# Turning the rounded values by block transposes and plain DMAs, and other places for early and last steps, in a fused attention and feed-forward kernel

## The chip, the cores and the metric

The kernel runs on one core of a Trainium2 chip. The time is that of the whole execution on the device in microseconds (us). The engines are TensorE (PE; PEld is its weight load), VectorE (DVE), ScalarE (ACT), GpSimd (POOL) and SyncE (SP), which here only issues DMAs. Each engine works through its own list of instructions in order; semaphores tie the lists together.

## The reference

The input x holds 16 sequences of 256 tokens with 256 channels. All is float32 except where said.

```
x = x + attention(layernorm(x))     16 query heads, 4 key/value heads of 128, softmax over
                                    the first 4 keys and the last 32, then the product with wo
x = x + ffn(layernorm(x))           one 256 x 256 linear layer in rounded integers:
  x_scale = max(max|h| / 127, 1e-12)      per token
  x_q = clip(round(h / x_scale), -128, 127)
  y = (x_q . w_q) * x_scale * w_scale + bias
```

The rounded integers fit bfloat16 exactly, so their product runs in bfloat16 on TensorE with sums in float32.

## The kernel before

**Tiling.** A sequence is two tiles of 128 tokens. A unit is one sequence, one group of four query heads and one tile: 8 units per sequence, 128 in all. The main loop goes once per unit; one pass is called a slot here. A slot's place in its sequence is its number modulo 8.

**Order.** Nothing is left to a scheduler: the function in_written_order (line 21) keeps every engine's instructions in the order in which Python writes them. What is done in a slot besides its own unit is put into lists by the function at (line 826): small (run at the end of the slot, and from unit 125 on, by line 938, already ahead of the normalisation), begin (after the scores), close (in the last unit) and others for keys, values, queries and the output projection.

**One slot.** TensorE makes the scores pss (line 560), a part of the output projection py (L678), the product po of the weights of two units earlier with the values (L623), in some slots the keys or values of the next sequence (pk L495, pv L507) and a pair of query heads (pq L527). Queries, keys, values and output projection go by a scheme with seven products instead of eight, so that VectorE or GpSimd must combine sums (lines 306 to 310, function combine). The query products of a slot lie in two PSUM banks; VectorE empties them in the next slot, L306 and L307 the first, L308 to L310 the second, and the queries of that slot are written to the same banks. VectorE further masks the scores (L571), takes their maximum (L573), normalises after ScalarE's exponentials (L605 to L617) and turns the weights in blocks of 32 x 32 (L582). A DMA out (zd, L584) and a DMA back (ad, L588) finish the turn; po reads ad two slots later. In the last units the turn is done by TensorE instead (ptd, L565), with a wait in the next slot.

**The steps of the rounded layer** (function ffn_steps, line 695, sequences 0 to 14): stats; norm (h = normalised x, L193); scale (xs, L714 and L715); quantise (L719 to L725: multiply and add a large constant on VectorE, clip and subtract it on GpSimd, result h16 in bfloat16); turn (L728, one DMA transpose by SP); linear (pa on TensorE L739, y on VectorE L744, the sum with x on GpSimd L745, the store on SP L746). They run in the next sequence's slots 4, 5, 6, 8, 9 and 10 after the sequence is done, so linear stands in slot 2 modulo 8, and norm, scale in 5 and 6. Sequence 14 has its own places near the end, and a seventh step that adds the bias (L733). The last sequence is done tile by tile (function last_steps, line 750): its d is rounded on VectorE (L778 to L784), turned by TensorE (ht_last, L791), multiplied (pa_last), scaled and stored.

**Turning the normalised x** (function turned_by_blocks, line 385, sequences 2 to 15): VectorE turns 32 x 32 blocks (L389), four DMAs write them to DRAM (L394) and four read them back into place (L403).

**Buffers.** x tiles rotate through 5 buffers (line 74); h, h16, hT and y have one each.

## Time and profile before

| | us |
|---|---|
| median of 3 runs (lowest, highest) | 769.09 (767.9, 769.29) |
| the profiled execution | 767.44 |
| its span, first to last instruction | 765.7 |
| TensorE busy in the span | 754.4 |
| VectorE | 621.8 |
| GpSimd | 511.7 |
| ScalarE | 399.2 |

The mean granted TensorE clock was 0.997. "Busy" counts the time in which an instruction runs; matmuls are pipelined, so two that follow each other overlap in the list. In the timelines a row has its start, its length, the engine, the line, the operation, out<-in by the program's names, shapes and a count; a bracket at the end tells how long the engine was idle before it, and what ended that.

### The profile page before, as it was taken

What the parts mean: (1) busy time and instruction counts of PE and PEld (TensorE: products, weight loads), DVE (VectorE), ACT (ScalarE), POOL (GpSimd) and SP (SyncE); (2) the same over time, 40 slices, a digit from 0 to 9 for tenths busy, and PEclk for the clock granted to TensorE, in tenths of its full rate; (3) what the DMA queues carried; (4) which work ended last, traced back from release to release, by engine and by line L of the source; (5) the groups of instructions that cost most, each with busy time, mean ns of one, the idle gap of its engine ahead of it and who ended that gap; (6) DMA issues with size and microseconds to landing.
All of it is one profiled execution on the core that took longest, in us unless ns stands there. A gap on an engine that the chain in (4) does not pass through costs nothing.

```text
span 765.7 us, 18824 instructions
## 1 busy us (share of the span) xinstructions
PE 754.4 (99%) x6483; PEld 742.4 (97%) x6483; DVE 621.8 (81%) x1775; ACT 399.2 (52%) x1561; POOL 511.7 (67%) x812
## 2 busy tenths in 40 slices
PE   9999999999999999999999999999999999999995
PEld 7999999999999999999999999999999999999994
DVE  2588888888888888888888888888888888778765
ACT  3555555555455454555555455554545555455551
POOL 4666977676675867757676675866758676675622
PEclk9999999999999999999999999999999999999998
DMA  7634354344544425445344543436344354443310
GB/s 241 215 102 129 106 147 140 107 124 118 154 124 133 131 90 163 128 137 144 100 125 128 147 141 123 129 96 163 120 145 135 99 136 128 130 137 105 100 40 31
DMA packets 150679, 97.45 MB, mean 127 GB/s; under 512 B 44984, under 2 KB 148792, under 8 KB 150584
## 3 DMA queue, kind: packets, MB, share of 16 engines
q1 hardware_dynamic: 150584, 96.24, 42.8%
q8 instruction: 52, 0.85, 0.5%
q14 instruction: 43, 0.35, 0.2%
HBM read 54.39 MB, written 39.85 MB: 123 GB/s over the span
## 4 chain that ended last, share of the span: by engine, by line
PE 96%; DVE 2%; DMA 1%; ACT 0%; POOL 0%; issue 0%; DVEq 0%; POOLq 0%; ACTq 0%
PE pq L527 24%; PE py L678 23%; PE po L623 15%; PE pss L560 14%; PE pk L495 6%; PE pv L507 6%; PE py L662 3%; PE pq L538 2%; PE pa L739 1%; DMA ad<-zd 1%; PE warm L891 1%; PE pv L470 0%; PE pk L461 0%; PE ptd L565 0%; ACT scores L598 0%
## 5 line engine op out<-in xcount | busy, mean ns | idle before, releaser
L598 ACT ACTIVATE scores<-scores,nmax 128x68 f32<-128x68 f32 x512 | 173.5, 340 | 247.2 <-DVE nmax L573 244.8
L623 PE MATMUL po<-ad,vw 96*128 96x128 f32 x1024 | 135.4, 275 | 0.4 <-DMA ad<-zd 0.4
L560 PE MATMUL pss<-kt,qt 128*128 128x68 f32 x1024 | 130.2, 268 | 0.0
L623 PEld LDWEIGHTS po<-ad,vw 96*128 96x128 f32 x1024 | 125.6, 192 | 1.5 <-DMA ad<-zd 0.5
L560 PEld LDWEIGHTS pss<-kt,qt 128*128 128x128 f32 x1024 | 126.1, 192 | 0.7 <-issue 0.5
L527 PE MATMUL pq<-xs,wq_sums 128*128 128x128 f32 x714 | 118.6, 275 | 0.0
L571 DVE SCALAR_TENSOR_TENSOR scores<-pss,masks 128x272 f32<-128x272 f32 x128 | 56.2, 439 | 63.7 <-PE pss L560 60.8
L527 PEld LDWEIGHTS pq<-xs,wq_sums 128*128 128x128 f32 x714 | 98.8, 192 | 0.0
L598 ACT ACTIVATION_READ_ACCUMULATOR scores<-scores,nmax 128x1 f32 x512 | 95.6, 187 | 0.0
L635 ACT COPY oT<-po 128x512 f32<-128x512 f32 x129 | 75.4, 585 | 23.0 <-PE po L623 23.0
L678 PE MATMUL py<-wo_sums,os 128*128 128x128 f32 x672 | 87.0, 279 | 0.0
L257 POOL TENSOR_TENSOR os<-oT 128x256 f32<-128x256 f32 x56 | 41.0, 732 | 58.0 <-ACT oT L635 58.0
L678 PEld LDWEIGHTS py<-wo_sums,os 128*128 128x128 f32 x672 | 79.5, 192 | 0.0
L306 POOL TENSOR_TENSOR ktmp<-b_k 128x256 f32<-128x256 f32 x30 | 22.4, 746 | 84.3 <-ACT b_k L327 84.3
L527 PE MATMUL pq<-xnT,wq_sb 128*128 128x128 f32 x476 | 72.7, 275 | 0.1
L582 DVE STREAM_TRANSPOSE z<-scores 128x384 f32<-128x384 f32 x120 | 69.4, 578 | 4.1
L617 DVE TENSOR_TENSOR scores<-scores,sm 128x272 f32<-128x272 f32 x120 | 60.3, 503 | 4.1
L527 PEld LDWEIGHTS pq<-xnT,wq_sb 128*128 128x128 f32 x476 | 62.7, 192 | 0.2 <-PE pv L507 0.2
L678 PE MATMUL py<-wo_sb,oT 128*128 128x128 f32 x448 | 62.0, 281 | 0.0
L573 DVE TENSOR_REDUCE nmax<-scores 128x4 f32<-128x272 f32 x128 | 55.8, 436 | 4.4
L678 PEld LDWEIGHTS py<-wo_sb,oT 128*128 128x128 f32 x448 | 54.5, 192 | 0.0
L308 DVE TENSOR_TENSOR qt<-pq,qt 128x256 f32<-128x256 f32 x119 | 50.5, 424 | 4.0
(187 smaller groups left out, 1700.4 us busy)
## 6 DMA issues: line engine op xcount, KB each, us to landing
zd<-z SPq DMA_DIRECT2D x120, 192.0 KB
ad<-zd SPq DMA_DIRECT2D x120, 192.0 KB
vd<-vt SPq DMA_DIRECT2D x30, 256.0 KB
vw<-vd SPq DMA_DIRECT2D x30, 256.0 KB
vw<-vd SPq DMA_DIRECT2D x30, 224.0 KB
x<-in_x_dram SPq DMA_DIRECT2D x15, 256.0 KB
out_dram<-y SPq DMA_DIRECT2D x15, 256.0 KB
zxd<-zx SPq DMA_DIRECT2D x56, 64.0 KB
```

The costliest lines, as they stand in the source:

```text
L308: eng.tensor_add(c21_c22, like(p[1][:, 0:2], c21_c22), v.unsqueeze(1).to_broadcast(c21_c22.shape))
L495: pe.matmul(to, left, right, start=True, stop=True)
L527: pe.matmul(to, left, right, start=True, stop=True)
L560: pe.matmul(pss[:, k, :], qt[n, g][:, t, k].rearrange("p h i -> p (h i)"), kt[n, g][:, t * NBLK + k, :], start=True, stop=True,)
L571: dve.scalar_tensor_tensor(s[:, :, 0:NK], pss, SCALE, masks[:, t], ALU.mult, ALU.add)
L573: dve.tensor_reduce(nmax, s[:, :, 0:NK], AX.X, ALU.max, negate=True)
L582: dve.transpose(z, s.rearrange("p k (c i) -> p c k i", c=NCH))
L598: act.activation(s[:, k, 0:NK], s[:, k, 0:NK], AF.Exp, bias=nmax[:, k : k + 1], scale=1.0, accum_out=sm[:, k : k + 1],)
L617: dve.tensor_mul(s, s, sm.unsqueeze(2).to_broadcast([P, NBLK, NK]))
L623: pe.matmul(po[:, k], vw[n, g // 2][:, t * NBLK + k, g % 2 * D : (g % 2 + 1) * D], ad[:, :, k], start=True, stop=True,)
L635: act.copy(o[:, t, hs].rearrange("p h (k i) -> p k h i", i=QB), po[:, :, hs])
L678: pe.matmul(region(py, i), left[:, e], right[:, e], start=(g == 0 and e == 0 and i in (1, 4)), stop=(g == G - 1 and e == 1 and i in (7, 3)),)
```

## The change

Four things change.

1. For sequences 0 to 13 the rounded values are no longer turned by one DMA transpose of a bfloat16 tile. They stay float32 (h, clipped and shifted in place), and go the way of the normalised x: a block transpose on VectorE, four DMAs out, four back (turned_by_blocks, made general), and a copy on ScalarE that narrows to bfloat16 (narrow). The steps are nine now, at slots 4, 5, 6, 8, 10, 11, 12, 13, 14 after the sequence's end; for sequence 13 at 4, 5, 6, 8, 9, 10, 11, 12, 13. The linear step so moves from slot 2 to slot 6 modulo 8, and to unit 125 for sequence 13. x tiles get a sixth buffer.
2. Sequence 14's values are turned by four bfloat16 transposes on TensorE.
3. In the last unit the matmuls of sequence 14's linear step are issued where they were, but their scaling, sum and store (rest) come after the rounding of the last sequence's first tile. x2's copy is issued earlier, and for the first tile its bias is added on GpSimd.
4. Early steps: the first sequence's transposes are copied out by halves on two engines, one half of sequence 2's norm moves from slot 5 to 6, and the rounding of the layer's weights from slot 9 to 8.

```diff
-    xp = ctx.enter_context(tc.tile_pool(name="xp", bufs=5))
+    xp = ctx.enter_context(tc.tile_pool(name="xp", bufs=6))
...
-    def turned_by_blocks(n):
+    def turned_by_blocks(src, pool_of, tag):
-        dve.transpose(z, xns[n].rearrange("p t (c q i) -> p q (t c) i", c=NC, q=NQ))
+        dve.transpose(z, src.rearrange("p t (c q i) -> p q (t c) i", c=NC, q=NQ))
...
-            (act.copy, dve.tensor_copy)[j](xnT[n][:, :, j * P : (j + 1) * P], pt)
+                (act.copy, dve.tensor_copy)[c](xnT[n][:, c, j * P : (j + 1) * P], pt[:, c])
...
-        h16 = p1.tile([P, NT, DM], BF, tag="h16", name=f"h16_{tag}")
+        h16 = p1.tile([P, NT, DM], BF, tag="h16", name=f"h16_{tag}") if n == B - 2 else h
...
+        way = []
+
         def turn():
-            sp.dma_start_transpose(
-                hT.rearrange("p j c t -> p (j c) t"), h16.rearrange("p j d -> p (j d)")
-            )
+            if n < B - 2:
+                way.extend(turned_by_blocks(h, p1, f"hb_{tag}"))
+                return
+            pt = ps_m.tile([P, NC, T], BF, tag="m", name=f"ht_{tag}")
+            for c in range(NC):
+                for j in tiles:
+                    pe.transpose(pt[:, c, j * P : (j + 1) * P], h16[:, j, c * P : (c + 1) * P], ident16)
+            way.append(pt)
+
+        def out():
+            way[0]()
+
+        def back():
+            way.append(way[1]())
+
+        def narrow():
+            act.copy(hT, way[-1])
...
-            for j in tiles:
-                dve.scalar_tensor_tensor(y[:, j, :], pa[:, j, :], xs[:, j : j + 1], wsc_bc, ALU.mult, ALU.mult)
-            pool.tensor_add(y, y, xt)
-            sp.dma_start(out_v[n], y)
+            def rest():
+                for j in tiles:
+                    dve.scalar_tensor_tensor(y[:, j, :], pa[:, j, :], xs[:, j : j + 1], wsc_bc, ALU.mult, ALU.mult)
+                pool.tensor_add(y, y, xt)
+                sp.dma_start(out_v[n], y)
+
+            return rest
-        return [stats, norm, scale, quantise, turn, linear, lambda: add_bias(dve)]
+        if n < B - 2:
+            return [stats, norm, scale, quantise, turn, out, back, narrow, linear]
+        return [stats, norm, scale, quantise, turn, narrow, linear, lambda: add_bias(dve)]
...
-            if j:
-                act.copy(x2, py)
+            act.copy(x2, py)
...
+            if j == 0:
+                pool.tensor_add(x2, x2, bias_bc)
...
-        places = (0, 1, 1, 2) if n == 1 else (4, 5, 6, 7) if n == 2 else (first - 2, first + 2, first + 4, first + 5)
+        places = (0, 1, 1, 2) if n == 1 else (4, 6, 6, 7) if n == 2 else (first - 2, first + 2, first + 4, first + 5)
...
-    for slot, f in zip((6, 9, 10, 10, 11, 12), ffn_weight_steps()):
+    for slot, f in zip((6, 8, 10, 10, 11, 12), ffn_weight_steps()):
...
-        slots = (4, 5, 6, 8, 9, 10) if n < B - 2 else (4, 5, 6, 6, 7, 7, 7)
+        slots = (4, 5, 6, 8, 10, 11, 12, 13, 14) if n < B - 2 else (4, 5, 6, 6, 7, 7, 7, 7)
+        if n == B - 3:
+            slots = (4, 5, 6, 8, 9, 10, 11, 12, 13)
         for k, slot in enumerate(slots):
-            def step(n=n, k=k):
+            def step(n=n, k=k, slot=done + slot):
                 if k == 0:
                     steps[n] = ffn_steps(n)
-                steps[n][k]()
-            at(done + slot, step, begin if k == 4 and n == B - 2 else close if k == 5 and n == B - 2 else small)
+                rest = steps[n][k]()
+                if rest and n == B - 2:
+                    at(slot, rest, close)
+                elif rest:
+                    rest()
+            if n < B - 2:
+                at(done + slot, step, begin if k in (5, 6) else small)
+            else:
+                at(done + slot, step, begin if k == 4 else close if k == 6 else small)
...
             tail = last_steps(0)
             for f in tail[:2]:
                 f()
+            for f in close.pop(i):
+                f()
```

More of the change, by code (lines that the diff above doesn't have):

```diff
@@ L383, in turned @@
         channels(n)
-    def turned_by_blocks(n):
-        z = p1.tile([P, NQ, NT * NC, QB], FP, tag="zx", name=f"zx_{n}")
-        dve.transpose(z, xns[n].rearrange("p t (c q i) -> p q (t c) i", c=NC, q=NQ))
-        zd = dram.tile([P, NQ, NT * NC, QB], FP, tag="zx", name=f"zxd_{n}")
+    def turned_by_blocks(src, pool_of, tag):
+        z = p1.tile([P, NQ, NT * NC, QB], FP, tag="zx", name=f"z_{tag}")
+        dve.transpose(z, src.rearrange("p t (c q i) -> p q (t c) i", c=NC, q=NQ))
+        zd = dram.tile([P, NQ, NT * NC, QB], FP, tag="zx", name=f"zd_{tag}")
         def out():
@@ L399, in back @@
         def back():
-            xnT[n] = p2.tile([P, NC, T], FP, tag="xnT", name=f"xnT_{n}")
+            to = pool_of.tile([P, NC, T], FP, tag=tag.split("_")[0], name=tag)
             for t in range(NT):
@@ L403, in back @@
                     sp.dma_start(
-                        xnT[n][:, c, t * P : (t + 1) * P].rearrange("p (a i) -> p a i", a=NQ), zd[:, :, t * NC + c]
+                        to[:, c, t * P : (t + 1) * P].rearrange("p (a i) -> p a i", a=NQ), zd[:, :, t * NC + c]
                     )
+            return to
         return out, back
@@ L698, in ffn_steps @@
         h = p1.tile([P, NT, DM], FP, tag="h", name=f"h_{tag}")
-        h16 = p1.tile([P, NT, DM], BF, tag="h16", name=f"h16_{tag}")
+        h16 = p1.tile([P, NT, DM], BF, tag="h16", name=f"h16_{tag}") if n == B - 2 else h
         xs = p2.tile([P, NT], FP, tag="xs", name=f"xs_{tag}")
-        hT = p1.tile([P, NT, NC, P], BF, tag="hT", name=f"hT_{tag}")
+        hT = p1.tile([P, NC, T], BF, tag="hT", name=f"hT_{tag}")
         y = p1.tile([P, NT, DM], FP, tag="yo", name=f"y_{tag}")
@@ L739, in linear @@
                     pe.matmul(
-                        pa[:, j, :], hT[:, j, c], wqfT[:, c, :],
+                        pa[:, j, :], hT[:, c, j * P : (j + 1) * P], wqfT[:, c, :],
                         start=(c == 0), stop=(c == NC - 1),
                     )
-            for j in tiles:
-                dve.scalar_tensor_tensor(y[:, j, :], pa[:, j, :], xs[:, j : j + 1], wsc_bc, ALU.mult, ALU.mult)
-            pool.tensor_add(y, y, xt)
-            sp.dma_start(out_v[n], y)
-        return [stats, norm, scale, quantise, turn, linear, lambda: add_bias(dve)]
+            def rest():
[7 more added lines that the diff above has]
+        return [stats, norm, scale, quantise, turn, narrow, linear, lambda: add_bias(dve)]
     def last_steps(j):
@@ L786, in turn @@
         def turn():
-            if not j:
-                act.copy(x2, py)
             for c in range(NC):
@@ L792, in turn @@
                 dve.tensor_scalar(hT[:, c], pt, MAGIC, None, ALU.subtract)
-            dve.tensor_add(x2, x2, bias_bc)
+            if j:
+                dve.tensor_add(x2, x2, bias_bc)
         def linear():
@@ L851, in turn @@
             def turn(n=n, slot=places[3]):
-                for k, f in enumerate(turned_by_blocks(n)):
-                    at(slot + 1 + k, f, begin)
+                out, back = turned_by_blocks(xns[n], p2, f"xnT_{n}")
+                at(slot + 1, out, begin)
+                at(slot + 2, lambda: xnT.__setitem__(n, back()), begin)
                 at(slot + 2, lambda: channels(n))
```

## The prediction

> **What bounds the kernel now.** I read the page's busy shares and chain first, then TensorE's waits, then one sequence cut at the first score matmul of each slot (a slot is one pass of the main loop; eight make a sequence, numbered 0 to 7; 10, 125 and 126 are counted from the start), then the timelines where the change touches a slot.

> ```profile
> PE 754.4 (99%) x6483; PEld 742.4 (97%) x6483; DVE 621.8 (81%) x1775; ACT 399.2 (52%) x1561; POOL 511.7 (67%) x812
> ...
> PE 96%; DVE 2%; DMA 1%; ACT 0%; POOL 0%; issue 0%; DVEq 0%; POOLq 0%; ACTq 0%
> ...
> 438.71:445.40 6.69, 6.69 (x62) 6.64 (x61) 4.60 (x12) 3.72 (x13) 6.32 (x11) 1.00 0.43 118
> ...
> 450.54:456.91 6.37, 6.37 (x58) 6.33 (x57) 5.96 (x20) 3.17 (x12) 4.07 (x6) 1.00 0.61 176
> ...
> 462.05:468.30 6.25, 6.25 (x58) 6.25 (x57) 5.92 (x16) 3.83 (x16) 4.11 (x6) 1.00 0.27 89
> ...
> 468.30:473.44 5.14, 5.14 (x49) 5.14 (x47) 3.69 (x12) 2.30 (x10) 2.79 (x6) 1.00 0.35 112
> ```

> TensorE is the bound. The windows (slots 2, 4, 6, 7: length, busy time, granted clock 1.00) show no idle, so in the body a moved step saves nothing; it can only make TensorE wait. Slot 2 is 0.44 us longer than slot 6: it holds the linear result (pa). Slot 4 is 0.12 us longer though nothing is added: there TensorE waits a little for VectorE.

> ```profile
> 399.50 0.87 DVE L744 SCALAR_TENSOR_TENSOR y<-pa,xs,wsc_bc 128x256 f32<-128x256 f32 x2 [1.59 <-PE pa L739]
> ...
> 400.34 0.44 DVE L571 SCALAR_TENSOR_TENSOR scores<-pss,masks 128x272 f32<-128x272 f32 x1
> ...
> 401.61 0.29 DVE L307 TENSOR_TENSOR qt<-pq,qt 128x128 f32<-128x128 f32 x1
> ...
> 402.59 0.29 DVE L310 TENSOR_TENSOR qt<-pq,qt 128x128 f32<-128x128 f32 x1
> ...
> 402.87 0.61 PE L527 MATMUL pq<-xnT,wq_sb 128*128 128x128 f32 x4
> ...
> 403.76 0.39 PE L527 MATMUL pq<-xs,wq_sb 128*128 128x128 f32 x2
> ...
> 421.14 0.68 DVE L714 TENSOR_REDUCE xs<-h 128x2 f32<-128x512 f32 x1
> ...
> 421.85 0.39 DVE L715 TENSOR_SCALAR xs<-xs 128x2 f32<-128x2 f32 x1
> ...
> 424.05 0.46 POOL L310 TENSOR_TENSOR vt<-b_v,vt 128x128 f32<-128x128 f32 x1
> ```

> The queries of a slot overwrite the two PSUM banks that VectorE empties in the same slot: the first after L307, the second after L310. In slot 3 above (starting 399.29) these end 0.96 us (402.87 - 401.90) and 0.88 us (403.76 - 402.88) ahead of the matmuls. That is the slack.

> ```profile
> 735.23 0.72 DVE L193 TENSOR_SCALAR h<-x,mv_f 128x256 f32<-128x256 f32 x2
> ...
> 737.30 0.69 DVE L611 TENSOR_TENSOR z<-scores,sm 128x384 f32<-128x384 f32 x1
> ...
> 737.34 1.06 PE L623 MATMUL po<-ad,vw 96*128 96x128 f32 x8
> ...
> 738.40 0.27 PE L565 MATMUL ptd<-ident,z 128*96 128x128 f32 x1
> ...
> 749.83 0.88 DVE L744 SCALAR_TENSOR_TENSOR y<-pa,xs,wsc_bc 128x256 f32<-128x256 f32 x2 [1.30 <-PE pa L739]
> ...
> 750.79 1.26 POOL L745 TENSOR_TENSOR y<-y,x 128x512 f32<-128x512 f32 x1 [5.98 <-DVE y L744]
> ...
> 752.13 0.19 POOL L768 TENSOR_SCALAR least_last<-mv_last 128x1 f32<-128x1 f32 x1
> ...
> 754.24 0.23 DVE L784 TENSOR_SCALAR d_last<-d_last 128x128 f32<-128x128 f32 x1
> ```

> The last fence is the end: z feeds ptd almost at once, and y with its sum stands before the last tile's rounding.

> **The change part by part.**

> *Turning by DMA, sequences 0 to 13.* One SP transpose (issue 1.25 us) goes; one VectorE block transpose (0.67 us, row L389), eight SP DMAs (1.93 + 3.50 us of issue, the rows of the same step for xn) and one ScalarE copy (0.59, as L635) come. The block transpose falls where VectorE idled 1.59 us before y. The copy stands ahead of p_q: it starts near 416.4, p_q ends near 417.2, and its reader L306 starts at 417.81: free. On SP the four "back" DMAs are in slot 4 behind ad, and push zd of that slot from 409.86 to about 410.8 (after ad at 407.2, 3.5 us of issue); its ad (412.01, near 413) still goes out some 5 us before its po (418.17), two slots on: free. If that cover went, po would wait as it once does, near 177 us (that slot took 6.88 us instead of 6.37). The "out" DMAs stand behind ad of slot 3. GpSimd's L725 writes f32 in place (as L724, 0.61 us instead of 1.52): relief, off the path. The sixth x buffer only keeps x until the later y.

> [...] The same rearranged step for xn ran in the window 436.5 to 440.5, some 4 us, against about 2 us for the transpose. [...]

> *y moves from slot 2/3 to 6/7, ahead of L714 and L715* (13 times: sequences 0 to 12). pa's 0.44 us moves along: zero for TensorE. y's sum on GpSimd (1.27) runs before os, which waits for oT anyway; its store on SP holds the next ad some 0.3 us (425.52 before), and po of that ad is 4 us off. In slot 3 y ends exactly when the scores are ready (400.34), so there it cost nothing. In slot 7 L714 (to the next start 0.71) and L715 follow y, before L571. Counted from the slot's start: y at 0.21, L714 at 1.00, L715 at 1.72. GpSimd's L310 then runs until 1.89 (424.51 - 422.19, less the 0.44 by which slot 6 grew); L715 took 0.39 where such an instruction ran and ended with it, 0.17 at 740.99 where none did. So L715 ends near 1.91 and L571 starts at 1.94 instead of 1.05: 0.89 late. From L571 to the ends of L307 and L310 take 1.56 and 2.54: 3.50 and 4.48, plus 0.15 until TensorE starts (slot 4: L307 ends 407.45, pk starts 407.60). The matmuls stand at 3.58 and 4.47: a wait of 0.07 and then 0.09. I take 0.16 x 13 = +2.1 us. Bounds: 0 (no wake-up time, 0.89 against 0.88) and 0.35 each (L715 a full 0.39), so 0 to 4.6.

> *Sequence 13's y in slot 125.* From unit 125 on the small steps stand before the normalisation. There y waits for pa, and h, sm, z stand behind it on VectorE; z is what the next slot's ptd waits for. From the slot's start (733.18): pa takes po's place at 4.16, y 0.64 later at 4.80, h at 5.59. h's second half meets GpSimd's y sum (1.26): where these two meet, rows grow (h 1.21 at 415.71 against 0.72 here). With the sum let through first, h ends near 7.35, z near 8.45 (sm, reciprocal 0.4, z 0.63); without, near 7.45. ptd stands at 5.66 (738.40 - 733.18 + 0.44 of pa). With 0.15 to wake: 1.9 to 2.9 us of idle TensorE. I take 2.9, as halves of h met so before. Nothing downstream absorbs it. [...]

> *Last chain.* Four bf16 transposes on TensorE replace the DMA: about 0.4 us (wt L227: 4 in 0.4), plus 0.1 since h16 is ready (744.80) just as they start. Rounding before y: the statistics start about 0.8 us sooner and the first GpSimd step no longer waits behind the 1.26 us sum, so d_last is ready near 752.9 instead of 754.47, even with the extra 0.5. But TensorE now reaches it only after po_3_1, near 753.2 (752.7 and the 0.5); its idle of 1.22 and 0.22 us closes. The two transposes end near 753.7, when the first half of oT is copied too; then py 0.87, pa_last 0.23, py 0.87: 755.8 instead of 756.7. y (0.84) falls between d_last and hT on VectorE: hT at 754.35, before pa_last's 754.6. The copy of x2, now ahead of ad_3_1 on ScalarE, ends near 750.2, before ptd's 750.5. Gain 0.8 (bounds 0.3, if x2's bias on GpSimd holds the rounding, to 1.4, the two idles closed).

> *Early steps.* The first sequence's copies by halves: pv starts at 6.12, the loads before it end at 5.88, so at most 0.1. xn's first half leaves slot 5's end: slot 6's waits (L307 ends 48.91, L310 49.90) shrink by 0.4, slot 7 gets 0.3 back. The weight rounding (1.62 us at 69.04) leaves the start of slot 10, where pv waits 0.3, for one with 1.32 us idle. In all -0.5 (bounds -0.9 and 0).

> Sum: 2.1 + 2.9 - 0.8 - 0.5 = +3.7 us. The profiled execution took 767.44 us (span 765.7), so 771.1 by it; the median of the runs, 769.09, is 1.65 above it, and by that **772.8 us**. Bounds: -0.4 and +7.2.

> **Rivals.**
> - *Slot 7 holds (chance 0.15).* The wait of 0.16 is near the reading error of 0.05 to 0.15. For it: slot 4 waits only 0.12 with VectorE 0.42 late. Against: 0.89 late exceeds the second slack. Then +1.6 (2.9 - 0.8 - 0.5): 770.7, or with z early 769.7.
> - *Faster (0.10).* One mechanism: y does not hold z in slot 125, and the slots hold. It decides if z is out before 5.66 in the slot. For it: L605 waits for ScalarE there until 736.89 anyway. Against: y stands ahead on VectorE and can't start before 4.80. Then -1.3 to -2.3: about 767.3.
> - *L715 misses the gap (0.10).* If it comes after L310 (margin 0.17 us) it waits for the whole y sum: 1.2 more, 13 x 1.36 = 17.7, so 788. For: xn at 46.55 (0.89 us) came 0.05 before such an end, missed it and waited through a second instruction. [...]
> - *DMAs late (0.05).* The 128-byte packets hold ad up and po waits 0.5 per sequence, as near 177 us: 13 x 0.5 + 3.7 = +10.2, 779.3. For: the DMA share of slot 0 is already 0.80. Against: ad goes out 4 to 5 us ahead.

> **How the numbers follow.** The forecast has 0.60, mostly above +1.5 us. About 0.2% (1.5 us) is what the measurement tells from no change. Slower: 0.55 of it, half of the first rival, and the last two: 0.77; faster 0.10; same 0.13. The range goes from the bound -0.4 to the bound +7.2, stretched a little to both sides: 768.3 to 777, leaving out most of the faster case and both late ones.

> **What would show it.** Slot 7 near 5.30 us with TensorE waiting for qt in L527, slot 3 at 5.14, slots 2 and 6 changing lengths (6.25, 6.69); one wait of 2 to 3 us of ptd for z near 738 us; the waits of ht_last for d_last down from three to that of the last tile (2.9 us); no wait for ad. Wrong if slot 7 stays at 5.14, if z in slot 125 comes before ptd, or if L715 takes over 1 us.

## The result, and the profile after

| | before | changed |
|---|---|---|
| median of 5 executions (lowest, highest), us | 768.0 (767.9, 769.29) | 775.93 (772.27, 777.7) |
| the profiled execution, us | 767.44 | 772.27 |
| its span, us | 765.7 | 770.5 |

The ratio is 1.0091 (95% interval 1.0075 to 1.0107): the changed kernel is some 7 us slower (the medians lie 7.9 apart), inside the range of the forecast and on the side it named, but twice as far from zero as the forecast (+3.7). The executions of the changed kernel also lie 5.4 us apart, those before 1.4; the profiled one is the fastest of its five. So one trace can't explain the median here, and the first experiment takes another.

The page of the changed kernel: busy time by engine, and the chain that ended last.

```profile
PE 756.2 (98%) x6487; PEld 743.6 (97%) x6487; DVE 626.1 (81%) x1789; ACT 405.0 (53%) x1577; POOL 515.0 (67%) x813
PE 95%; DVE 2%; DMA 1%; issue 0%; ACT 0%; POOL 0%; DVEq 0%; POOLq 0%; ACTq 0%
```

TensorE still bounds it. It has 1.8 us more work, the rest is new idle time. TensorE's waits tell which (total, times, longest), first of the changed kernel, then of the one before. (Lines from 423 on stand one further down than before, later ones more: L571 is L572 now, L714 and L715 are L715 and L716, L744 is L763.)

```profile
PE ht_last L813 <- DVE d_last L808: 3.5, 2, 3.3
PE ptd L566 <- DVE z L612: 2.6, 1, 2.6
PE po L624 <- DMA ad<-zd: 1.8, 2, 1.4
PE xt L423 <- ACT xnT L424: 0.7, 2, 0.4
```

```profile
PE ht_last L791 <- DVE d_last L784: 4.3, 3, 2.9
PE po L623 <- DMA ad<-zd: 0.4, 1, 0.4
```

Two of the four were forecast (z, and less waiting for d_last in all). Two were not: po waits for ad, and at the very start xt waits for its copies. The short waits of slot 7 stay below what this view lists; they show in the windows of slots 2, 4, 6 and 7 of one sequence (length, then PE, PEld, DVE, ACT, POOL busy, clock, DMA share, GB/s):

```profile
441.31:447.57 6.26, 6.26 (x59) 6.26 (x58) 5.20 (x13) 3.29 (x12) 5.98 (x10) 1.00 0.31 81
452.70:459.07 6.37, 6.37 (x59) 6.33 (x57) 5.96 (x20) 3.17 (x12) 4.08 (x6) 1.00 0.78 209
464.20:470.89 6.69, 6.69 (x62) 6.64 (x61) 5.00 (x14) 4.36 (x17) 4.47 (x7) 1.00 0.27 92
470.89:476.14 5.25, 5.25 (x48) 5.24 (x47) 4.77 (x15) 2.14 (x10) 3.40 (x6) 1.00 0.46 133
```

pa's 0.44 us has gone from slot 2 to slot 6 and cancels out; slot 7 takes 5.25 instead of 5.14. The rows of that slot 7, which starts at 470.89:

```profile
471.10 0.88 DVE L763 SCALAR_TENSOR_TENSOR y<-pa,xs,wsc_bc 128x256 f32<-128x256 f32 x2 [1.59 <-PE pa L756]
471.89 0.68 DVE L715 TENSOR_REDUCE xs<-h 128x2 f32<-128x512 f32 x1
472.32 0.46 POOL L310 TENSOR_TENSOR vt<-b_v,vt 128x128 f32<-128x128 f32 x1
472.60 0.21 DVE L716 TENSOR_SCALAR xs<-xs 128x2 f32<-128x2 f32 x1
472.72 0.43 DVE L572 SCALAR_TENSOR_TENSOR scores<-pss,masks 128x272 f32<-128x272 f32 x1
```

The masking of the scores (L572) comes 1.83 us into the slot, behind y, L715 and L716; before it came at 1.04.

The other new wait is that of po for ad. What SP issues in slot 7, first in the kernel before, then in the changed kernel, where y's store stands ahead of ad, with the late po of slot 40:

```profile
332.31 0.37 SPq L512 DMA_DIRECT2D vd<-vt  x1
332.73 0.46 SPq L94 DMA_DIRECT2D x<-in_x_dram  x1
333.30 0.43 SPq L588 DMA_DIRECT2D ad<-zd  x1
```

```profile
239.33 0.38 SPq L513 DMA_DIRECT2D vd<-vt  x1
239.77 0.46 SPq L94 DMA_DIRECT2D x<-in_x_dram  x1
240.57 0.38 SPq L765 DMA_DIRECT2D out_dram<-y  x1
241.04 0.42 SPq L589 DMA_DIRECT2D ad<-zd  x1
245.51 1.16 PE L624 MATMUL po<-ad,vw 96*128 96x128 f32 x8 [0.44 <-DMA ad<-zd]
```

Below, "landing" is the time from the start of ad's issue to the end of its last packet, and "slack" what is then left until po is due. The semaphore that po waits for came 0.3 to 0.8 us after the last packet in these two kernels (slots 0 from 16 to 104), so the margin that po really had is smaller than the slack: 0.8 to 1.1 us in the kernel before, 0.35 to 0.8 in the changed kernel where po did not wait.

With every slot cut at its first score matmul, the difference to the kernel before is complete, in the profiled execution and in the second one (label again, below):

| where | forecast | profiled execution | second execution |
|---|---|---|---|
| slot 7, 13 times | +2.1 | +1.4 | +1.3 |
| slot 126, wait for z | +2.9 | +2.75 | +2.75 |
| slot 126, half clock behind that wait | not in it | 0 | +1.66 |
| po waits for ad (slots 0 and 28) | 0 | +1.9 | +3.3 |
| up to the first score | -0.1 | +0.4 | +2.55 |
| slots 6, 7 and 10 of the early part | -0.4 | -0.4 | -0.4 |
| from the last slot's scores to the end | -0.8 | -1.2 | -1.2 |
| sum | +3.7 | +4.8 | +9.9 |

The sums are those of the spans: 770.5 and 775.6 against 765.7.

### The profile page after: what moved, and what is told of

The parts are those of the page before. It is cut to its first block, busy times and chain, and to the rows that moved or that the text cites. A ratio compares the mean times of both kernels' runs of the same rounds, so it can differ in the third digit from the quotient of the medians.

```text
span 770.5 us, 19062 instructions
## 1 busy us (share of the span) xinstructions
PE 756.2 (98%) x6487; PEld 743.6 (97%) x6487; DVE 626.1 (81%) x1789; ACT 405.0 (53%) x1577; POOL 515.0 (67%) x813
## 4 chain that ended last, share of the span: by engine, by line
PE 95%; DVE 2%; DMA 1%; issue 0%; ACT 0%; POOL 0%; DVEq 0%; POOLq 0%; ACTq 0%
PE pq L528 24%; PE py L679 23%; PE po L624 15%; PE pss L561 14%; PE pk L496 6%; PE pv L508 6%; PE py L663 3%; PE pq L539 2%; DMA ad<-zd 1%; PE pa L756 1%; PE warm L924 1%; PE pk L462 0%; PE pv L471 0%; PE ptd L566 0%; DVE h L193 0%
## 5 line engine op out<-in xcount | busy, mean ns | idle before, releaser
L572 DVE SCALAR_TENSOR_TENSOR scores<-pss,masks 128x272 f32<-128x272 f32 x128 | 56.1, 438 | 65.0 <-PE pss L561 62.4
L257 POOL TENSOR_TENSOR os<-oT 128x256 f32<-128x256 f32 x56 | 43.4, 776 | 62.5 <-ACT oT L636 62.5
L306 POOL TENSOR_TENSOR ktmp<-b_k 128x256 f32<-128x256 f32 x30 | 22.4, 748 | 80.6 <-ACT b_k L327 80.6
```

The source lines that it names most:

```text
L572: dve.scalar_tensor_tensor(s[:, :, 0:NK], pss, SCALE, masks[:, t], ALU.mult, ALU.add)
```

## The experiments

Each was run beside the kernel before. Medians of the kernel before were 768.3, 768.5, 768.05 and 768.9 us in the four groups of runs. A time here is the median, with lowest and highest; "first score" is the start of the first score matmul.

**again: the changed kernel once more.** No edit.

> The changed kernel once more, as the yardstick for the runs beside it. Three costs were read from its first trace: 13 short waits in slot 7 (5.25 us instead of 5.14, 1.4 us), one wait of ptd for z in slot 126 (2.75 us), and waits of po for ad in slot 0 (1.9 us in that execution, 0.5 for one such wait before). Theory 'late ad': the first two come back to 0.05 us, the third differs from execution to execution, so the times lie 3 us or more apart, between 771 and 778, median 774 to 777. Rival 'constant cost': all executions near 772.3, spread below 1.5 us as before.

Measured: 775.24 us (774.24 to 779.79, 6 executions), ratio 1.0100 (1.0079 to 1.0121). The theory of late ads holds, but it is not the whole: slot 126 did not come back. It took 9.89 us instead of 8.23. The windows show why (the clock is the third number from the end); the first is the wait itself, TensorE busy for 0.43 of 3 us:

```profile
744.90:747.90 3.00, 0.43 (x5) 0.32 (x4) 2.69 (x6) 0.58 (x1) 1.36 (x1) 1.00 0.14 47
747.90:748.90 1.00, 1.00 (x8) 1.00 (x9) 0.00 (x0) 0.00 (x0) 0.00 (x0) 0.60 0.36 120
748.90:749.90 1.00, 1.00 (x6) 0.91 (x6) 0.44 (x2) 0.26 (x1) 0.00 (x0) 0.50 0.00 0
749.90:750.90 1.00, 1.00 (x4) 0.82 (x3) 1.00 (x2) 0.79 (x4) 0.00 (x0) 0.50 0.00 0
750.90:751.90 1.00, 1.00 (x4) 0.80 (x4) 0.90 (x5) 0.98 (x6) 0.00 (x0) 0.69 0.00 0
```

After the wait the granted clock was 0.50 for 3.4 us (0.8 + 1 + 1 + 0.62), at a cost of 1.66. In the first trace the same wait of 2.6 us left it at 1.00. Three later traces with that wait (store_later, linear_later, load_later) show the half clock too, slot 126 taking 9.83, 9.91 and 9.86: four of five. Only the order of events was seen, so the wait is the likely cause; the run y_after_z tests it.

What sets the first trace apart stands in the clock record of the traces. The first stretches at full clock last 737.28, 754.35, 757.76, 761.17 or 768.00 us; they differ by 3.41 us or multiples of it, and are 216, 221, 222, 223 or 225 times 3.413. So the changes of the granted clock in these traces stand on a grid of 3.413 us, which lay differently from trace to trace (full clock from 5.83 in the first, from 10.82 in this one). In the four traces with the half clock, 2.50 to 2.57 us of the wait fall between two grid points; the clock drops at the second of them, for one step of 3.413 us. In the first trace a grid point (743.11) lies in the middle of the wait and parts it into 1.29 and 1.28 us. That this spared it is the author's reading of five traces.

The second new item is at the start: TensorE in the profiled execution, then in this one.

```profile
5.80 0.44 PE L423 MATMUL xt<-ident,xn 128*128 128x128 f32 x2 [0.36 <-ACT xnT L424]
6.60 0.33 PE L423 MATMUL xt<-ident,xn 128*128 128x128 f32 x1 [0.36 <-ACT xnT L424]
6.76 1.89 PE L471 MATMUL pv<-wv_sb,xnT 128*128 128x512 f32 x4
```

```profile
5.80 0.69 PE L423 MATMUL xt<-ident,xn 128*128 128x128 f32 x2 [0.36 <-ACT xnT L424]
6.85 0.47 PE L423 MATMUL xt<-ident,xn 128*128 128x128 f32 x1 [0.36 <-ACT xnT L424]
7.11 3.62 PE L471 MATMUL pv<-wv_sb,xnT 128*128 128x512 f32 x4
```

The two waits of 0.36 us for ScalarE's copy are in both, and in no trace with whole copies: cut into halves, the second transpose of a tile waited until the first half was copied. In the second execution the matmuls ran at half pace until 10.5 us (the four of pv took 3.62 instead of 1.89), and the first score came at 17.58 instead of 15.39. The clock record begins, at full clock, at 10.82 us here and at 10.30 in early_only, which shows the half pace too; in the other twelve traces it begins at 4.8 to 7.0. The same grid tells them apart. Counted back one step from the first entry, a grid point stood at 7.41 here (6.89 in early_only), and the step that ended there held both waits, 0.72 us of idle TensorE; full clock came one step later. In the other six traces with half copies the step at whose end full clock came held 0.36 us of these waits at most.

**store_later: y's store behind slot 7's ad.**

```diff
-                sp.dma_start(out_v[n], y)
+                if n < B - 3:
+                    at((n + 1) * PER + 15, lambda: sp.dma_start(out_v[n], y), begin)
+                else:
+                    sp.dma_start(out_v[n], y)
```

> Only the store of y is moved, from ahead of slot 7's ad on SP to behind slot 7's own begin steps, so behind that ad. Theory 'store': the 256 KB store shares the transfer engines with that ad, which then lands 3.0 to 3.2 us after its issue instead of 2.5 to 2.7, and leaves 0.7 to 0.9 us before po instead of 1.3 to 1.6. With the store behind, the landing is back at 2.4 to 2.7 us, po waits for ad at most once, the times lie within 1.5 us, and the median is 768.0 + 1.4 + 2.75 - 1.2 = 771.0 (770.3 to 771.8). Rival 'packets': the added 128-byte packets of the turn slow every transfer; then nothing changes: median 774 to 777, spread 3 us or more.

Measured: 773.14 us (771.76 to 773.31), ratio 1.0059 (1.0047 to 1.0071): 2.1 less than the changed kernel beside it, and a spread of 1.5 instead of 5.5. One wait of 0.6 for ad was left. The theory of the store holds and the rival of the small packets falls, since those are all still there. Two numbers missed: 773.1 instead of 771.0, mostly because slot 126 had the half clock (1.66) that the expectation left out; and the landing, which stayed at 2.5 to 3.2 us. The slack came from the issue instead: ad now goes out 4.56 us before po is due, in the changed kernel 3.87, in the kernel before 4.03.

**y_after_z: sequence 13's y behind z.**

```diff
-                if rest and n == B - 2:
+                if rest and n == B - 3:
+                    at(slot, rest, later)
+                elif rest and n == B - 2:
                     at(slot, rest, close)
```

> Only the scaling, sum and store of sequence 13 are moved, from ahead of h, sm and z in unit 125 to behind z in the same unit. Theory 'y holds z': slot 126 goes from 8.23 to 5.5 us (ptd no longer waits, or under 0.3), and the median falls by 2.3 to 2.75 us against the run of the changed kernel beside it. [...] Rival 'handed on': y after z delays the scores of slot 126, which then takes 6 us or more, and only 1.5 to 2.2 us come back.

Measured: 771.59 us (769.42 to 775.58, 7 executions), ratio 1.0048 (1.0028 to 1.0068), 3.65 us less than the changed kernel beside it. Its window of slot 126:

```profile
741.27:746.75 5.48, 5.48 (x39) 5.07 (x37) 4.04 (x11) 2.61 (x10) 2.53 (x3) 1.00 0.14 48
```

The slot is back at 5.48 with the clock at 1.00. So y ahead of h and z was the cause, and y behind z makes TensorE wait for nothing new. More came back than the wait of 2.75, which fits a half clock of 1.66 that most executions had and now have not. The late ads and the half copies are still in it, and its executions lie 6.2 us apart.

**linear_later: the linear step of sequences 0 to 12 in slot 1 of the next sequence.**

```diff
-        slots = (4, 5, 6, 8, 10, 11, 12, 13, 14) if n < B - 2 else (4, 5, 6, 6, 7, 7, 7, 7)
+        slots = (4, 5, 6, 8, 10, 11, 12, 13, 17) if n < B - 2 else (4, 5, 6, 6, 7, 7, 7, 7)
```

> For sequences 0 to 12 the linear step with y, sum and store is moved from slot 6 to slot 1 of the next sequence (y at the start of slot 2, where nothing stands on VectorE ahead of the scores). Theory 'y and L714/L715 together': slot 7 is back at 5.14 us, slot 2 stays at 6.25, slot 1 takes 5.58 with pa: 1.4 us less. Theory 'store': ad of slot 7 lands after 2.4 to 2.7 us again and the times lie within 1.5 us. Together 768.0 + 2.75 - 1.2 = 769.6 (769.0 to 770.5). Rival 'packets': the spread stays and the median is 772.5 or more. Rival 'any slot': y makes TensorE wait in slot 2 too (slot 2 above 6.30).

Measured: 772.49 us (770.57 to 773.24), ratio 1.0050 (1.0037 to 1.0062). Slot 7 took 5.14, slot 2 stayed at 6.25, slot 1 took 5.57, and no po waited for ad in a slot 0 (landing 2.4 to 2.7 us, but 3.4 and 3.5 in slots 32 and 96): theory one as expected, and theory two but for its spread, which is 2.7 us instead of 1.5. The median is 2.9 above the expectation. In its trace, the fastest of the five executions, 1.7 us are the half clock in slot 126 (9.91 us) and some 0.8 are short waits in slots 5, 28, 59, 83 and 122, whose cause is open except in slot 28 (a late ad). The rest of the median is not explained.

**early_only: the kernel before with the early steps alone**, the three edits of the change's fourth part.

```diff
-            (act.copy, dve.tensor_copy)[j](xnT[n][:, :, j * P : (j + 1) * P], pt)
+                (act.copy, dve.tensor_copy)[c](xnT[n][:, c, j * P : (j + 1) * P], pt[:, c])
...
-        places = (0, 1, 1, 2) if n == 1 else (4, 5, 6, 7) if n == 2 else (first - 2, first + 2, first + 4, first + 5)
+        places = (0, 1, 1, 2) if n == 1 else (4, 6, 6, 7) if n == 2 else (first - 2, first + 2, first + 4, first + 5)
...
-    for slot, f in zip((6, 9, 10, 10, 11, 12), ffn_weight_steps()):
+    for slot, f in zip((6, 8, 10, 10, 11, 12), ffn_weight_steps()):
```

> The kernel before with the early steps of the change alone (copies by halves, half of xn moved, weight rounding moved). In the first trace of the change these gave +0.37 us up to the first score, -0.06 in slots 6 and 7 and -0.36 in slot 10, -0.05 in all. In the second execution the matmuls after the two waits of the halves (0.36 us each) ran at half pace until 10.5 us and the first score came at 17.58 instead of 15.39, 2.2 us later. Theory 'half pace': that is due to those waits and comes in most executions: median 769.0 to 770.6, the times 2 us or more apart, some of them near 770.5. Rival 'chance of the chip': the halves cost 0.37 and nothing more: median 768.0 to 768.5, spread 2 us at most, as before.

Measured: 768.22 us (767.03 to 770.72, 12 executions), ratio 1.0005 (0.9995 to 1.0015). Neither theory had the median right. Four of the twelve lie at 770.07 to 770.72, the other eight at 767.03 to 768.71, and the profiled one (770.07) shows the half pace, first score at 17.32. So by the times it comes in about a third of the executions. Those without it are a little faster than before, as slot 10 (6.64 instead of 7.00) promises. Of the eight traces with half copies two had the half pace; of the six with whole copies (first score at 14.6 to 15.3) none.

**last_only: the kernel before with the last units alone** (parts 2 and 3 of the change; sequences 0 to 13 keep the DMA transpose, their slots and five x buffers). Against the changed kernel, besides the early steps undone:

```diff
-                way.extend(turned_by_blocks(h, p1, f"hb_{tag}"))
+                sp.dma_start_transpose(
+                    hT.rearrange("p j c t -> p (j c) t"), h16.rearrange("p j d -> p (j d)")
+                )
...
-            return [stats, norm, scale, quantise, turn, out, back, narrow, linear]
+            return [stats, norm, scale, quantise, turn, linear]
...
-        slots = (4, 5, 6, 8, 10, 11, 12, 13, 14) if n < B - 2 else (4, 5, 6, 6, 7, 7, 7, 7)
-        if n == B - 3:
-            slots = (4, 5, 6, 8, 9, 10, 11, 12, 13)
+        slots = (4, 5, 6, 8, 9, 10) if n < B - 2 else (4, 5, 6, 6, 7, 7, 7, 7)
```

> The kernel before with the last units of the change alone (sequence 14 turned by TensorE, rounding of the last sequence's first tile ahead of sequence 14's y). Theory: the end is 1.2 us shorter, as read from the last score to the end (20.79 against 21.99 us): median 768.3 - 1.2 = 767.1 (766.6 to 767.6). Rival: the gain is tied to the late slot 126 of the changed kernel, in which VectorE and ScalarE get ahead; then 0.5 or less: median 767.8 or more.

Measured: 767.35 us (766.85 to 768.48, 11 executions), ratio 0.9988 (0.9980 to 0.9997). The gain is there by itself: 20.98 us from the last slot's scores to the end instead of 21.96.

**before_store7: the kernel before, y's store held back to the end of slot 6.** Nothing else moves; y is long ready then.

```diff
-            sp.dma_start(out_v[n], y)
+            if n < B - 2:
+                at((n + 1) * PER + 14, lambda: sp.dma_start(out_v[n], y))
+            else:
+                sp.dma_start(out_v[n], y)
```

> The kernel before, with only the store of y held back to the place it has in the changed kernel (end of slot 6, ahead of slot 7's ad on SP); y, pa and the transpose stay where they were. Theory 'store': ad of slot 7 lands 2.9 to 3.2 us after issue instead of 2.4 to 2.7, po waits for it in one to four of the slots 0, 0.3 to 1.7 us each, and the median is 769.0 to 771.5. Rival 'store and small packets together': landing under 2.8 us, no more waits than before, median 768.3 within 0.5.

Measured: 777.99 us (777.53 to 781.38), ratio 1.0136 (1.0119 to 1.0154). The store alone, moved by four slots, costs more than the whole change. TensorE's waits in the profiled execution, which is the slowest of the four, and SP's issues in one slot 7 (slot 7 starts at 334.96, slot 0 at 340.10):

```profile
PE po L623 <- DMA ad<-zd: 11.3, 12, 2.1
```

```profile
337.30 0.37 SPq L512 DMA_DIRECT2D vd<-vt  x1
337.73 0.46 SPq L94 DMA_DIRECT2D x<-in_x_dram  x1
338.24 0.49 SPq L747 DMA_DIRECT2D out_dram<-y  x1
338.82 0.41 SPq L588 DMA_DIRECT2D ad<-zd  x1
```

The order is to be read here: vd waits 3.2 us on SP for GpSimd's vt, and x (256 KB), y (256 KB) and ad (192 KB) leave in one go behind it. po is due 2.23 us into slot 0, that is 3.50 us after ad's issue (4.03 before). From 340.10 to 343.00 the DMA share was 0.96 (the first transfers of vw among them), and po ran at 344.04, 1.7 late. The expectation went up to +3, measured is +9.5: it took over the landing seen in the changed kernel. There ad has 0.37 us more, because vd hangs on the values made early in slot 6, and pa makes that slot 0.44 longer behind them.

**repaired: the changed kernel with whole copies, linear in slot 1 and y behind z** (the edits of linear_later and y_after_z, and the first sequence's copies as they were).

```diff
-                (act.copy, dve.tensor_copy)[c](xnT[n][:, c, j * P : (j + 1) * P], pt[:, c])
+            (act.copy, dve.tensor_copy)[j](xnT[n][:, :, j * P : (j + 1) * P], pt)
```

> The changed kernel with three things put right: the first sequence's copies whole again, the linear step of sequences 0 to 12 in slot 1 (as in the run before), y of sequence 13 behind z. The turning by blocks and DMAs stays. If the waits found are all there is: 768.3 - 1.2 (end) - 0.42 (xn half, weight rounding) + 0.4 (small waits seen in slots 28, 59, 83, 122 of the run before) = 767.1 (766.3 to 768.0), first score at 15.0, slot 126 at 5.48, clock 1.00 throughout the body. Rival 'the DMA way itself costs': 769 or more, with waits of po for ad.

Measured: 767.62 us (766.85 to 768.62, 11 executions), ratio 0.9995 (0.9986 to 1.0004), inside the expected range. All the blocks, small packets and extra copies of the turning are in it, but so are the gains of the last units and of two early steps. The kernel with the last units and the weight rounding alone (best1, below) stands at 0.9979 (0.9969 to 0.9989). So the turning together with linear in slot 1 may still cost about a microsecond: 1.2 by the ratios, 0.6 by the medians, with intervals that just overlap. Some 0.3 of it is in the trace, as short waits in slots 59, 83 and 122, which linear_later has too and the changed kernel has not.

**sum_later: sequence 13's sum and store at the end of unit 126.**

```diff
-                pool.tensor_add(y, y, xt)
-                sp.dma_start(out_v[n], y)
+                def add_store():
+                    pool.tensor_add(y, y, xt)
+                    sp.dma_start(out_v[n], y)
+                if n == B - 3:
+                    at((n + 1) * PER + 14, add_store, later)
+                else:
+                    add_store()
```

> The changed kernel; only GpSimd's sum and the store of sequence 13 move, from unit 125 to the end of unit 126. y stays ahead of h on VectorE. Two things are asked. First, how much of the wait in slot 126 is the sum's: with it h took 1.68 us (two halves), in the kernel before 0.72. Theory 'shared port': h is back at 0.72, ptd waits 1.6 us instead of 2.6 and slot 126 takes 7.2 to 7.4 us where the clock is 1.00 (8.2 with the sum). Rival: h stays above 1.2 us, the wait at 2.2 or more. Second, the clock: in three of four executions with the wait of 2.6 us the granted clock was 0.50 for some 3.4 us behind it, and slot 126 took 9.8 to 9.9 us. If a wait of 1.6 us does that too, slot 126 takes 8.8 or more and the median is 1 us under that of the changed kernel (774 to 775); if not, it is 2.6 us under it (772 to 773.5).

Measured: 773.62 us (771.51 to 775.76, 6 executions), ratio 1.0069 (1.0054 to 1.0084). VectorE and GpSimd ahead of slot 126's wait in the changed kernel, then VectorE and TensorE here:

```profile
740.79 0.88 DVE L763 SCALAR_TENSOR_TENSOR y<-pa,xs,wsc_bc 128x256 f32<-128x256 f32 x2 [2.66 <-PE pa L756]
741.59 1.68 DVE L193 TENSOR_SCALAR h<-x,mv_f 128x256 f32<-128x256 f32 x2
741.75 1.36 POOL L764 TENSOR_TENSOR y<-y,x 128x512 f32<-128x512 f32 x1 [4.94 <-DVE y L763]
743.58 0.67 DVE L612 TENSOR_TENSOR z<-scores,sm 128x384 f32<-128x384 f32 x1
```

```profile
741.51 0.73 DVE L193 TENSOR_SCALAR h<-x,mv_f 128x256 f32<-128x256 f32 x2
742.55 0.67 DVE L612 TENSOR_TENSOR z<-scores,sm 128x384 f32<-128x384 f32 x1
743.37 0.29 PE L566 MATMUL ptd<-ident,z 128*96 128x128 f32 x1 [1.62 <-DVE z L612]
```

h takes 0.73 us without the sum beside it and 1.68 with it: 0.95 of the wait is the sum's, 1.62 is y's own. The rows show these lengths alone; for why h takes longer beside the sum, 'shared port' is the author's name, and no run shows the cause. Slot 126 took 7.28 with the clock at 1.00. The median lies between the two expectations on the clock, and one trace doesn't say how often the clock is halved behind a wait of 1.6 us: open. In this trace a grid point of the clock (742.85) parts the wait into 1.10 and 0.52 us.

**load_later: the changed kernel with x's load behind slot 7's ad, the store still ahead.**

```diff
-            at(max(first - 4, 0), lambda n=n: load_x(n))
+            at(max(first - 3, 0), lambda n=n: load_x(n), begin if first > 4 else small)
```

> The changed kernel with the load of x (256 KB) moved behind slot 7's ad; the store of y (256 KB) stays ahead of it. Theory 'what is queued ahead of that ad decides, load or store alike': ad lands 2.4 to 2.7 us after its issue again (3.0 to 3.2 with both ahead), po waits for it at most once, and the median is 772.5 to 774 against 775.2 to 775.9 of the changed kernel, as it was with the store moved instead (773.1). Rival 'the store, being a write to DRAM like zd and vd, is what hurts': landing stays near 3.0 us, two or more waits, median 774.5 or more.

Measured: 772.58 us (771.91 to 774.04), ratio 1.0060 (1.0046 to 1.0073); landing 2.3 to 3.2 us, 3.5 and 3.6 in the two slots 0 that lost time, 0.5 us together. The medians with the load moved (772.6) and with the store moved (773.1) are alike: either of them between vd and ad on SP counts, not which.

**best1: the kernel before with the last units and the weight rounding in slot 8.** Against last_only:

```diff
-    for slot, f in zip((6, 9, 10, 10, 11, 12), ffn_weight_steps()):
+    for slot, f in zip((6, 8, 10, 10, 11, 12), ffn_weight_steps()):
```

> The kernel before with the last units of the change and the weight rounding in slot 8, nothing else. 768.5 - 1.1 (as measured for the last units) - 0.36 (slot 10) = 767.0 (766.5 to 767.4), first score at 15.0 in every execution, so no times 2 us above the rest. Rival: the weight rounding gives nothing in the median: 767.35.

Measured: 766.59 us (765.84 to 767.44, 8 executions), ratio 0.9979 (0.9969 to 0.9989). Both gains add up.

**best2: best1, half of xn in slot 6, and x's load behind slot 7's ad** (the edit of load_later). Against best1:

```diff
-        places = (0, 1, 1, 2) if n == 1 else (4, 5, 6, 7) if n == 2 else (first - 2, first + 2, first + 4, first + 5)
+        places = (0, 1, 1, 2) if n == 1 else (4, 6, 6, 7) if n == 2 else (first - 2, first + 2, first + 4, first + 5)
...
-            at(max(first - 4, 0), lambda n=n: load_x(n))
+            at(max(first - 3, 0), lambda n=n: load_x(n), begin if first > 4 else small)
```

> As the run beside it, plus half of xn from slot 5 to 6 (-0.06) and the load of x (256 KB) moved from ahead of slot 7's ad to behind it. Theory 'what is queued ahead of that ad decides': its issue comes 0.5 us earlier, it lands within 2.2 us, the slack before po goes from 1.3-1.6 to 2.2 us or more, no po waits in a slot 0, and the median falls by the 0.5 to 0.9 us that such waits took in the profiled executions: 766.0 to 766.6, spread 1.2 us at most. Rival: the waits come from the code fetches alone, whatever is ahead: median as the run beside it within 0.2.

Measured: 765.31 us (764.74 to 765.76), ratio 0.9961 (0.9949 to 0.9973). SP in slot 7:

```profile
470.03 0.37 SPq L513 DMA_DIRECT2D vd<-vt  x1
470.56 0.34 SPq L589 DMA_DIRECT2D ad<-zd  x1
470.96 0.51 SPq L94 DMA_DIRECT2D x<-in_x_dram  x1
```

ad goes out 4.49 us before po is due, no slot 0 waits, and the spread is 1.0 us. It beats both kernels: all its executions lie below all those of best1. The median is 0.7 below the expected range. Against best1's trace, the waits for ad give 0.95 us (slots 28, 64 and 108); another 0.54 came behind the last scores and 0.2 ahead of the first, and nothing here shows that the swap makes these. One wait of 0.5 us is left, in slot 28.

**What makes a late ad late.** In the profiled execution po waited in slots 40 and 64 only, though the slack was 0.7 to 0.9 us in most. The transfers from ad's issue (241.04) to po (245.51) have one of a kind that most slots 0 have not (packets, MB, share of the 16 transfer engines):

```profile
q1 hardware_dynamic: 1162, 0.98, 74.7%
q8 instruction: 1, 0.02, 1.3%
```

It is of the kind that the page calls instruction (a fetch, below): one packet of 16,384 bytes that started at 243.06 and took 0.96 us while ad's packets were under way. The last of these came singly, up to 244.99; of the 16 updates of ad's semaphore 15 had come by 244.43, the last came at 245.47. In slot 64 of that execution the delay can be seen itself: 368 of ad's 384 packets had ended by 383.57, a fetch ran from 383.42 to 384.37, and the next packet of ad ended at 384.43; 15 updates had come by 383.91, the last came at 385.79. In the second execution it was so in slot 64 (366 packets by 385.32, fetch 385.18 to 386.13, next packet 386.20) and in slot 88 (365 by 525.56, fetch 525.11 to 526.17, next packet 526.25).

The thirteen traces other than before_store7 have 169 slots 0 between slots 16 and 112. In 64 such a fetch began between ad's issue and po's time, and in 17 of these po waited (0.28 to 1.83 us). In the 105 without a fetch none waited over 0.03 us. The slots 4 have eight waits (in 28 and 108, the 0.5 us of the kernel before among them), and all eight had a fetch too. The fetches stand in the same slots 0 in all these traces (16, 40, 64, 88 and 112; in the kernel before not in 16), so the count alone could also speak for something else in these slots; the packets' times above speak for the fetch. When the fetch comes after ad's issue varies: in slot 64 from 1.98 to 3.30 us. So a slack that suffices in most slots is no cover where a fetch falls. Between the two traced executions of the changed kernel the late ads make 1.4 of 5.1 us; their share in the spread of the others is not known. In before_store7 ad is late without them. That the fetch held up the one part in sixteen that came last is the author's reading of these times.

## Why the prediction was right, and where it was not

- *What bounds it, pa's move for nothing, the turning free where it stands*: right, as far as the runs tell. The table of the first trace is complete without a term for the turning; by repaired and best1 it costs about a microsecond, if anything.
- *Slot 7, +2.1*: right in mechanism, 1.4 in size. y ended, L715 followed at 1.00, L716 at 1.71 us of the slot, each as worked out. The masking of the scores came at 1.83 instead of 1.94, as it starts 0.09 before L716 ends; the wait is 0.11 per slot. The rivals "slot 7 holds" and "L715 misses the gap" fell.
- *Slot 125, +2.9*: right to 0.15, and its two parts (y itself, and h beside GpSimd's sum) are shown by y_after_z and sum_later. What the step lacked is what comes behind a wait: "nothing downstream absorbs it" was true, but in four of five traces the half clock added 1.66 to it, where the clock's grid did not part the wait.
- *The store, "holds the next ad some 0.3 us, and po of that ad is 4 us off"*: this step failed. The 4 us were right (ad was issued 3.87 us before po), but they were never held against the time that ad takes to land, and this was taken as unchanged when 256 KB more stood in front of it. Landing went from 2.4-2.7 to 2.7-3.2 us and the slack from 1.3-1.6 to 0.7-0.9; up to the semaphore the margin went from some 0.9 to some 0.4, too little beside a fetch of 1 us. Waits that were put at nothing took 1.9 and 3.3 us more than before in the two traces. The rival "DMAs late" had the right waiter with the wrong cause and size: it spoke of the 128-byte packets and of 0.5 us in each of 13 sequences (+6.5). Two and four of those slots 0 waited in the two traces, and store_later, load_later and repaired, which keep the packets, lost 0.5 to 0.8 us there. It was given 0.05.
- *Early steps, -0.5*: failed at the first sequence's copies. They were taken as a gain of at most 0.1; they made two waits of 0.36 us in every trace that has them, since the second transpose of a tile waited for the first half's copy; the first score came 0.1 to 0.4 later by it, and some 2.2 more in about a third of the executions, where full clock came one step of its grid later. The other two (-0.06 and -0.36) came as forecast.
- *Last chain, -0.8*: 1.2 in the changed kernel, 1.0 alone. Mis-sized within its bounds.
- *The row of xn's step, some 4 us against about 2 us for the transpose*: the first trace has no wait that the longer way makes. By blocks and plain DMAs the turning costs about a microsecond here, if anything (1.2 by the ratios, 0.6 by the medians).

That the median lies in the range is luck in part. The range's upper bound came mostly from slot 7 (0.35 us each time), which took less than forecast; what filled it are late ads, the half clock and the late start, and none of them had a term. The forecast of 772.8 also stood on a median before of 769.09 from three executions; with five it was 768.0, from which the forecast difference of 3.7 leads to 771.7, and the miss is 4.2 us instead of 3.1.

By the terms in the table the median's 7 us are: 1.4 in slot 7, 2.75 + about 1.3 in slot 126 (four of five), 2 to 3 of late ads, 0.4 + about 0.7 at the start (one of three), less 0.4 and 1.2. That is 7 to 8. The shares taken over the executions are estimates from few traces.

## What to carry to other kernels

Of a step that is moved, hold each transfer's landing time up to its semaphore, with everything queued ahead of it at the new place, against the moment its reader is due, and ask for a microsecond or two more than the median landing: po waited 0.28 to 1.83 us in 17 of the 64 slots 0 where an instruction fetch fell here, at places that nobody chose. Count a new TensorE wait of some 2.5 us at more than its length: behind one of 2.6 us the clock was 0.50 for 3.4 us in four of five traces here, 1.66 us more. Be careful also with small waits at the start: 0.72 us of them went with a first score some 2.2 us later in two of eight traces. When executions spread further than before, take a second trace ahead of explaining the first.
